# Sorting edges by node on one core: three of five comparisons on VectorE, ScalarE's comparisons earlier, and a folding of weights in sixteen steps

## The chip, the cores and the metric

The kernel runs on one core of a Trainium2 chip. The metric is the device time of one execution in microseconds (us); the figure for a kernel is the median of several executions. The core has five engines with a queue of instructions each, which they work off in order: PE (TensorE, matrix products; the loads of its stationary operand are listed apart as PEld), DVE (VectorE), ACT (ScalarE), POOL (GpSimd) and SP (SyncE, here only an issuer of transfers). Transfers run on 16 DMA engines beside them.

## The reference

A graph with 6250 nodes and 206250 edges. Every edge row of 128 numbers is added to the row of its source node; node rows, sums and one global row go through three layers with softplus between; the input is added and each row is normalised.

```python
edge_aggr = jnp.zeros((n, HIDDEN), dtype=x.dtype).at[row].add(edge_features)
global_expand = jnp.repeat(global_feat, reps, axis=0)
combined = jnp.concatenate([x, edge_aggr, global_expand], axis=-1) @ W_c + b_c
h = jax.nn.softplus(combined @ W1 + b1)
h = jax.nn.softplus(h @ W2 + b2)
return h @ W3 + b3
...
x = _layernorm(x + _L0_gnn_ref(x, edge_index, edge_attr_128, ...))
```

## The kernel before

**What is done.** The edges are sorted by source node in order to be summed with dense products. The nodes fall into 32 buckets of 196. The edges stand in 1692 columns of 122 (846 pairs of columns). For each column a one-hot matrix `sort_hot` is made that moves each of its edges to a slot; PE multiplies it with the edge rows (`gather`, line 1153, into a PSUM bank `sorted`), ScalarE copies the product into one of six sets of pairs (`settle`, line 1165), and GpSimd scatters one pair at a time to a table in device memory ordered by bucket, `rows_by` (`scatter_row`, line 1182, an indirect DMA of 256 rows). Once enough scatters are through, a chunk of 128 rows of one bucket is certain to be full: SP loads it back (`chunks`, line 293), VectorE compares its node numbers with 0 to 195 (`match`, `hot`, line 990), and PE multiplies chunk and `hot` and adds up in a PSUM tile `part` (`product`, line 1013), which VectorE adds to the sums (`sums_t`, line 1036). After the last scatter the last chunks of all buckets are summed, and the three node layers run bucket range by bucket range (lines 1356 to 1437).

**Pieces.** The 846 pairs stand in eight groups (28, 72, 124, 124, 124, 128, 124 and 122 pairs), and each group in pieces of up to three pairs, 286 pieces in all. A piece has up to six columns. Its `sort_hot` is made by one of two engines: VectorE compares all six columns in one operation (line 1137; one operand, `slot_ps`, lies in PSUM), ScalarE takes one operation a column, the distance |slot - place| (line 1140), and a last one over all six, relu(1 - distance) (line 1142). The slots themselves come from VectorE and PE, a group ahead (`positions`, lines 498 to 764).

**What sets the order.** PE, VectorE, ScalarE and SP run in an order written out by hand. Every step is entered with a nominal time and the steps are then issued in order of that time: `SCATTER` = 1.3 places is a scatter, so a piece of three pairs begins 3.9 places after the one before. For a piece that begins at t, VectorE's comparison is entered at t - 17.5 (`COMPARED`), ScalarE's operations at t - 17.5 - `SPREAD` and then every 0.65 places, PE's products at t - 14 and t - 12.05, and ScalarE's copies at t - 10.5 and t - 8.55. The nominal times give only the order; when a step runs is decided by its engine's queue and by the data. An engine whose next step waits does nothing else.

**Buffers.** `sort_hot` has three buffers, given out in the order in which the comparisons are issued; `hot` has six; the banks `sorted` three, `small` two and `part` two; the sets of pairs six; the loaded chunks six.

**The folding.** Weights and biases are multiplied out once (`node_rows`): `fold`, the first layer's weights for node rows and sums; `z_bias`, `b2_c` and `b3_all`, the three layers' biases. The bias chain has four small products, each needing VectorE's result of the one before. Two steps, `combine` and `biases`, hold all of it; `over` spreads them over the last 15% of the fourth group.

Of the kernel before, what the change touches and what calls it, by code (L numbers as in the profile page):

```python
# [7 lines left out]
F32 = mybir.dt.float32  # L8
# [6 lines left out]
ALU = mybir.AluOpType  # L15
# [3 lines left out]
P = 128  # L19
# [127 lines left out]
def kernel(  # L147
# [21 lines left out]
    nc = tc.nc  # L169
    N, D = n_nodes, x.shape[2]  # L170
# [89 lines left out]
    ones = const.tile([P, P], F32, name="ones")  # L260
# [9 lines left out]
    cols = of_weights["cols"]  # L270
# [45 lines left out]
    def small_bank():  # L316
        return ps.tile([P, 4, P], F32, name="small", bufs=2)

    with ExitStack() as phase:
        rows_p = phase.enter_context(tc.tile_pool(name="rows", bufs=ROWS))  # L320
        sort_p = phase.enter_context(tc.tile_pool(name="sort", bufs=3))
        pairs_in = phase.enter_context(tc.tile_pool(name="pairs_in", bufs=2))
        per = phase.enter_context(tc.tile_pool(name="per", bufs=2))
        keep = phase.enter_context(tc.tile_pool(name="keep", bufs=1))
# [740 lines left out]

        def node_rows():

            steps = []

            def combine():  # L1070


                small = small_bank()
                nc.tensor.matmul(small[:, 0, :1], of_weights["wc2"], cols[:, 3:4],
                                 start=True, stop=True)
                nc.vector.tensor_add(c_bias, small[:, 0, :1], cols[:, 0:1])
                small = small_bank()
                for k in range(2):
                    nc.tensor.matmul(small[:, k, :], of_weights[f"wc{k}"], w_sb["w1"],
                                     start=True, stop=True)  # L1080
                nc.vector.tensor_copy(fold, small[:, :2, :])

            def biases():
                small = small_bank()
                nc.tensor.matmul(small[:, 0, :1], w_sb["w1"], c_bias, start=True, stop=True)
                nc.vector.tensor_add(z_bias, small[:, 0, :1], cols[:, 1:2])

                nc.vector.tensor_scalar(neg_z, z_bias, -1.0, None, op0=ALU.mult)
                small = small_bank()
                nc.tensor.matmul(small[:, 0, :1], w_sb["w2"], z_bias, start=True, stop=True)  # L1090
                nc.vector.tensor_add(b2_c, small[:, 0, :1], cols[:, 2:3])
                nc.vector.tensor_scalar(neg_b2, b2_c, -1.0, None, op0=ALU.mult)
                b2_all = per.tile([P, P], F32, name="b2_all", bufs=1)
                nc.vector.tensor_scalar(b2_all, ones, b2_c, None, op0=ALU.mult)
                small = small_bank()
                nc.tensor.matmul(small[:, 0, :], b2_all, w_sb["w3"], start=True, stop=True)
                nc.vector.tensor_add(b3_all, small[:, 0, :], of_weights["b3"])
# [33 lines left out]
        def compare(i):  # L1131
            g, c, m = pieces[i]
            slot, at = slot_of[g], 2 * (c - groups[g][0])
            assert all((g, at + j) in slots_done for j in range(2 * m))
            hot = hot_of[i] = sort_p.tile([P, 2 * PAIRS, P], F32, name="sort_hot")
            if i % SHARE == 0:
                return [lambda: nc.vector.tensor_tensor(  # L1137
                    hot[:PN, :2 * m], slot[:PN, at:at + 2 * m].unsqueeze(2).to_broadcast([PN, 2 * m, P]),
                    slot_ps[:PN].unsqueeze(1).to_broadcast([PN, 2 * m, P]), op=ALU.is_equal)]
            return [lambda j=j: nc.scalar.activation(  # L1140
                hot[:PN, j], by_slot[:PN], AF.Abs, bias=slot[:PN, at + j:at + j + 1], scale=-1.0)
                for j in range(2 * m)] + [lambda: nc.scalar.activation(  # L1142
                    hot[:PN, :2 * m], hot[:PN, :2 * m], AF.Relu, bias=1.0, scale=-1.0)]
# [50 lines left out]
        with tc.manual_schedule(engines={ET.PE, ET.DVE, ET.Activation, ET.SP}):  # L1194
# [71 lines left out]
            for i, t in enumerate(begins):  # L1266
                mine = units(i)
                soon = 0.0 if i else SOON
                if i % SHARE == 0:
                    when(t - COMPARED - soon, lambda i=i: compare_next(i))  # L1270
                else:
                    for j in range(2 * pieces[i][2] + 1):
                        when(t - COMPARED - SPREAD + j * SCATTER / 2, lambda i=i: compare_next(i))
                for u, unit in enumerate(mine):
                    late_by = SCATTER * pieces[i][2] * u / len(mine)
                    soon = 0.0 if i or u else SOON
                    when(t - GATHERED + late_by - 1.7 * soon, lambda unit=unit: gather(unit))
                    when(t - SETTLED + late_by, lambda unit=unit: settle(unit))
# [338 lines left out]
```

## Time and profile before

| | us |
|---|---|
| median of 3 executions (1283.15 to 1290.0) | 1289.03 |
| the profiled execution | 1289.92 |
| its span | 1288.2 |

Busy time in that span: PE 1167.7 us (91%), DVE 1027.6 (80%), ACT 1003.9 (78%), POOL 880.9 (68%); the mean granted TensorE clock was 0.962 of full speed. The rows of the profile name source line, engine and operation, then the output tile, an arrow and the inputs. A "group" gives busy time and mean length of one, and the idle time of that engine just before it with what ended it. One product of 32-bit numbers appears as two records of PE. A "wait" row gives total us, number of times, and the longest. Idle time of an engine that nobody waits for costs nothing, and a busy PE may be a PE whose products are drawn out.

### The profile page before, as it was taken

The page shows a single profiled execution, that of the slowest core. Times are in us where ns is not written, and L with a number is a line of the kernel's source. Part 1 is how long each engine was busy: PE and PEld are TensorE (multiplying, and loading weights), DVE is VectorE, ACT ScalarE, POOL GpSimd, SP SyncE. Part 2 cuts the span into 40 slices and gives each one's busy share as a digit, 9 for nine tenths or more (in the row PEclk, how much of TensorE's full clock was granted, in tenths as well). Part 3 has the DMA queues.
Part 4 walks back from the last instruction along what each step waited for, and adds up shares of the span by engine and source line. Part 5 has one row for each costly group of instructions (what it writes and reads, how often), then busy time and mean ns, then how long its engine had stood idle before and what let it go on. Part 6 is the DMA issues. An engine that isn't in the chain of part 4 may idle for free.

```text
span 1288.2 us, 26304 instructions
## 1 busy us (share of the span) xinstructions
PE 1167.7 (91%) x8617; PEld 1111.8 (86%) x8617; DVE 1027.6 (80%) x2260; ACT 1003.9 (78%) x2335; POOL 880.9 (68%) x915
## 2 busy tenths in 40 slices
PE   5778898888998998999899999999999999899893
PEld 5667788877988898989899999999999999898772
DVE  7868977888789977899878887789876767687784
ACT  5897987899687888977998888988899999403343
POOL 2777777777577776776777777777777777750334
PEclk9788998989999998999999999999999999999996
DMA  6789998899999997997999999999999999874421
GB/s 248 240 296 347 344 334 288 305 344 355 339 327 331 362 330 278 319 325 246 322 309 309 323 336 328 345 313 335 316 350 334 369 336 363 288 218 140 140 75 53
DMA packets 174636, 381.96 MB, mean 297 GB/s; under 512 B 27546, under 2 KB 118626, under 8 KB 160670
## 3 DMA queue, kind: packets, MB, share of 16 engines
q1 hardware_dynamic: 130751, 260.70, 61.2%
q0 software_dynamic: 41328, 115.65, 23.1%
q10 hardware_dynamic: 2415, 3.85, 0.9%
q8 instruction: 72, 1.18, 0.4%
q14 instruction: 70, 0.57, 0.1%
HBM read 242.47 MB, written 142.20 MB: 299 GB/s over the span
## 4 chain that ended last, share of the span: by engine, by line
PE 65%; DVE 12%; ACT 8%; DMA 7%; issue 4%; POOL 3%; SPq 0%; ACTq 0%; DVEq 0%; POOLq 0%
PE part L1013 37%; PE sorted L1153 21%; ACT pairs L1165 4%; DMA rows_by<-pairs,pair 4%; POOL rows_by L1182 3%; ACT sort_hot L1140 3%; DMA chunks<-rows_by 3%; DVE hot L990 2%; DVE past L727 1%; PE small L557 1%; PE small L559 1%; ACT sort_hot L1142 1%; DVE sort_hot L1137 1%; DVE sums_t L1036 1%; PE small L1395 1%
## 5 line engine op out<-in xcount | busy, mean ns | idle before, releaser
L1182 POOL DMA_INDIRECT rows_by<-pairs,pair x846 | 828.1, 979 | 298.3 <-issue 202.8
L1013 PE MATMUL part<-hot,chunks 128*128 128x196 f32 x3516 | 675.1, 335 | 13.2 <-DVE sums_t L1036 9.9
L1165 ACT COPY pairs<-sorted 64x387 f32<-64x387 f32 (+2 forms) x1144 | 542.6, 474 | 118.8 <-PE sorted L1153 95.7
L1013 PEld LDWEIGHTS part<-hot,chunks 128*128 128x128 f32 x3516 | 582.0, 193 | 21.9 <-DVE sums_t L1036 11.3
L1153 PE MATMUL sorted<-rows,sort_hot 122*128 122x129 f32 x3384 | 498.5, 288 | 44.5 <-ACT sort_hot L1142 32.0
L1153 PEld LDWEIGHTS sorted<-rows,sort_hot 122*128 122x128 f32 x3384 | 457.6, 199 | 53.5 <-ACT sort_hot L1142 36.3
L990 DVE TENSOR_TENSOR hot<-chunks,both_ps 128x784 f32<-128x784 f32 (+3 forms) x541 | 426.1, 809 | 9.2 <-DMA chunks<-rows_by 9.0
L1140 ACT ACTIVATE sort_hot<-plain,slot 122x128 f32<-122x128 f32 x840 | 292.8, 394 | 18.6 <-PE sorted L1153 6.3
L1036 DVE TENSOR_TENSOR sums_t<-sums_t,part 128x392 f32<-128x392 f32 (+1 forms) x262 | 143.5, 548 | 134.0 <-PE part L1013 133.0
L1137 DVE TENSOR_TENSOR sort_hot<-slot,both_ps 122x768 f32<-122x768 f32 x143 | 134.5, 940 | 1.9 <-PE sorted L1153 1.0
L1142 ACT ACTIVATE sort_hot<-sort_hot 122x768 f32<-122x768 f32 x143 | 118.6, 830 | 3.9
L1437 POOL TENSOR_SCALAR y<-y,mv,rs 128x128 f32<-128x128 f32 x40 | 31.1, 785 | 93.8 <-DVE rs L1425 93.5
L576 DVE TENSOR_REDUCE slot<-small 122x16 f32<-122x512 f32 (+2 forms) x109 | 72.9, 668 | 21.5 <-PE small L559 20.7
L1367 ACT ACTIVATE away<-sorted,z_bias 128x512 f32<-128x512 f32 (+2 forms) x13 | 8.5, 656 | 72.9 <-PE sorted L1357 72.9
L498 DVE TENSOR_TENSOR pair_ib<-pair_block,plain 122x512 bf16<-122x512 bf16 (+2 forms) x157 | 63.4, 411 | 0.2
L557 PE MATMUL small<-pair_ib,half 122*122 122x512 bf16 (+2 forms) x109 | 43.3, 398 | 7.6 <-DVE slot L576 7.5
L742 PEld LDWEIGHTS <-past 128*128 128x128 f16 x424 | 25.4, 100 | 17.9 <-DVE past L727 12.7
L727 DVE TENSOR_TENSOR past<-both_ps,starts 128x512 f16<-128x512 f32 (+1 forms) x61 | 39.8, 664 | 1.2 <-PE small L742 0.9
L742 PE MATMUL small<-jump,past 128*128 128x56 f16 (+3 forms) x424 | 29.4, 190 | 11.8 <-DVE past L727 8.4
L559 PEld LDWEIGHTS <-starts_h 128*122 128x122 bf16 x236 | 25.3, 148 | 11.9 <-issue 7.7
L1114 ACT COPY rows<-pair_i 122x16 f32<-122x16 f32 x106 | 22.2, 209 | 17.0 <-DMA rows<-in_edge 16.4
L727 DVE TENSOR_TENSOR past<-both_ps,starts_late 128x512 f16<-128x512 f32 (+2 forms) x49 | 32.3, 661 | 0.0
(163 smaller groups left out, 515.6 us busy)
## 6 DMA issues: line engine op xcount, KB each, us to landing
rows<-in_edge SPq DMA_DIRECT2D x105, 1032.0 KB
chunks<-rows_by SPq DMA_DIRECT2D x362, 136.0 KB
chunks<-rows_by SPq DMA_DIRECT2D x203, 204.0 KB
chunks<-rows_by SPq DMA_DIRECT2D x75, 272.0 KB
rows_by<-pairs,pair POOLq DMA_INDIRECT x846
rows_by<-fill SPq DMA_DIRECT2D x10, 1249.5 KB
rows_by<-fill SPq DMA_DIRECT2D x10, 714.0 KB
chunks<-rows_by SPq DMA_DIRECT2D x13, 408.0 KB
```

The source lines that it names most:

```text
L498: nc.vector.tensor_tensor(ib, cols.unsqueeze(2).to_broadcast([PN, m, SB, QUAD]), bucket_at[:PN].unsqueeze(1).to_broadcast([PN, m, SB, QUAD ...
L576: nc.vector.tensor_reduce(to, of, axis=mybir.AxisListType.X, op=ALU.max)
L727: nc.vector.tensor_tensor(past[:, :, a:b], twice_ps[:KB].unsqueeze(1).unsqueeze(1).to_broadcast([KB, 2, b - a, P // 2]), own["starts"][:, ...
L990: nc.vector.tensor_tensor(hot[:, q - a:q - a + m], chunks[j][:, lo:hi + 1:step, D:W].to_broadcast([P, m, BL]), iota_ps.unsqueeze(1).to_bro ...
L1013: nc.tensor.matmul(part[:, b - base_of[v], :], t[:, place_in(j, q), :D], hot[:, q - a], start=first, stop=last)
L1036: nc.vector.tensor_add(here, here, of)
L1137: return [lambda: nc.vector.tensor_tensor(hot[:PN, :2 * m], slot[:PN, at:at + 2 * m].unsqueeze(2).to_broadcast([PN, 2 * m, P]), slot_ps[:P ...
L1140: return [lambda j=j: nc.scalar.activation(hot[:PN, j], by_slot[:PN], AF.Abs, bias=slot[:PN, at + j:at + j + 1], scale=-1.0) for j in rang ...
L1142: for j in range(2 * m)] + [lambda: nc.scalar.activation(hot[:PN, :2 * m], hot[:PN, :2 * m], AF.Relu, bias=1.0, scale=-1.0)]
L1153: nc.tensor.matmul(out[:, j, :], hot[:PN, at], rows_at[col // LOAD_COLS][:PN, col % LOAD_COLS, :], start=True, stop=True)
L1165: nc.scalar.copy(sets_at[i][64 * n:64 * n + 64, lo:lo + m, h, :W], out[64 * h:64 * h + 64, :m, :])
L1182: s = nc.gpsimd.indirect_dma_start(out=dst, out_offset=bass.IndirectOffsetOnAxis(ap=at, axis=0), in_=rows[:, j].rearrange("p a b -> p (a b ...
```

## The change

A few numbers and one function change. `BY_ACT` = (1, 3) of `SHARE` = 5: of five pieces the second and fourth are compared by ScalarE and the other three by VectorE, where the engines took turns. `SPREAD` grows from 2.0 to 4.5, so that ScalarE's operations are entered 22 places ahead of the piece. `sort_hot` gets a fourth buffer, `hot` gives up its sixth. The folding is cut into sixteen steps, three of them empty.

```diff
-SHARE, SPREAD = 2, 2.0
+BY_ACT, SHARE, SPREAD = (1, 3), 5, 4.5
...
-    hots = ctx.enter_context(tc.tile_pool(name="hots", bufs=6))
+    hots = ctx.enter_context(tc.tile_pool(name="hots", bufs=5))
...
-        sort_p = phase.enter_context(tc.tile_pool(name="sort", bufs=3))
+        sort_p = phase.enter_context(tc.tile_pool(name="sort", bufs=4))
...
-            return [combine, biases]
+            banks_of, v = {}, nc.vector
+
+            def product_of(name, *pairs):
+                small = banks_of[name] = small_bank()
+                for k, (of, by, w) in enumerate(pairs):
+                    nc.tensor.matmul(small[:, k, :w], of, by, start=True, stop=True)
+
+            def got(name, k=0, w=1):
+                return banks_of[name][:, k, :w]
...
+            return [
+                lambda: product_of("c", (of_weights["wc2"], cols[:, 3:4], 1)),
+                lambda: product_of("fold", *((of_weights[f"wc{k}"], w_sb["w1"], D) for k in range(2))),
+                lambda: v.tensor_add(c_bias, got("c"), cols[:, 0:1]),
+                lambda: v.tensor_copy(fold, banks_of["fold"][:, :2, :]),
+                lambda: product_of("z", (w_sb["w1"], c_bias, 1)),
+                lambda: None,
+                lambda: v.tensor_add(z_bias, got("z"), cols[:, 1:2]),
+                lambda: v.tensor_scalar(neg_z, z_bias, -1.0, None, op0=ALU.mult),
+                lambda: product_of("b2", (w_sb["w2"], z_bias, 1)),
+                lambda: None,
+                lambda: v.tensor_add(b2_c, got("b2"), cols[:, 2:3]),
+                lambda: v.tensor_scalar(neg_b2, b2_c, -1.0, None, op0=ALU.mult),
+                b2_rows,
+                lambda: product_of("b3", (b2_all[0], w_sb["w3"], D)),
+                lambda: None,
+                lambda: v.tensor_add(b3_all, got("b3", w=D), of_weights["b3"]),
+            ]
...
-            if i % SHARE == 0:
+            if i % SHARE not in BY_ACT:
...
-                if i % SHARE == 0:
+                if i % SHARE not in BY_ACT:
                     when(t - COMPARED - soon, lambda i=i: compare_next(i))
```

How this moves the instructions, at two places. ScalarE, in the middle of the scatter stage (`pairs_108` to `pairs_113` are the six sets; a piece has four copies, its comparison six operations that read `plain` and `slot` and a last one on `sort_hot` alone); before:

```order
L1165 COPY pairs_110<-sorted 64x3x129 x4
L1114 COPY rows<-pair_i 122x16
L1140 ACTIVATE sort_hot<-plain,slot 122x128 x2
L1165 COPY pairs_111<-sorted 64x3x129 x2
L1140 ACTIVATE sort_hot<-plain,slot 122x128 x3
L1165 COPY pairs_111<-sorted 64x3x129 x2
L1140 ACTIVATE sort_hot<-plain,slot 122x128
L1142 ACTIVATE sort_hot<-sort_hot 122x768
L1165 COPY pairs_112<-sorted 64x3x129 x4
```

and with the change (lines are two higher):

```order
L1167 COPY pairs_111<-sorted 64x3x129 x2
L1116 COPY rows<-pair_i 122x16
L1167 COPY pairs_112<-sorted 64x3x129 x2
L1142 ACTIVATE sort_hot<-plain,slot 122x128 x3
L1167 COPY pairs_112<-sorted 64x3x129 x2
L1142 ACTIVATE sort_hot<-plain,slot 122x128 x3
L1167 COPY pairs_113<-sorted 64x3x129 x2
L1144 ACTIVATE sort_hot<-sort_hot 122x768
L1167 COPY pairs_113<-sorted 64x3x129 x2
L1167 COPY pairs_108<-sorted 64x3x129 x4
```

The comparison that stood among the copies of one piece now begins among those of one piece and ends among those of the next, and there are pieces whose copies follow with no comparison between.

PE at the folding; before:

```order
L1074 MATMUL small<-weights_sb 128x1
L1079 MATMUL small<-weights_sb 128x128 x2
L1153 MATMUL sorted<-rows,sort_hot 128x129 x3
L1013 MATMUL part<-hot,chunks 128x196 x4
L1153 MATMUL sorted<-rows,sort_hot 128x129 x2
L1013 MATMUL part<-hot,chunks 128x196 x4
L1153 MATMUL sorted<-rows,sort_hot 128x129 x6
L1013 MATMUL part<-hot,chunks 128x196 x7
L1153 MATMUL sorted<-rows,sort_hot 128x129 x9
L1085 MATMUL small<-c_bias,weights_sb 128x1
L1090 MATMUL small<-z_bias,weights_sb 128x1
L1096 MATMUL small<-weights_sb,b_all 128x128
```

and with the change, from the third small product on:

```order
L1073 MATMUL small<-c_bias,weights_sb 128x1
L1155 MATMUL sorted<-rows,sort_hot 128x129 x3
L1013 MATMUL part<-hot,chunks 128x196 x4
L1155 MATMUL sorted<-rows,sort_hot 128x129 x2
L1013 MATMUL part<-hot,chunks 128x196 x4
L1155 MATMUL sorted<-rows,sort_hot 128x129 x6
L1013 MATMUL part<-hot,chunks 128x196 x3
L1073 MATMUL small<-z_bias,weights_sb 128x1
L1013 MATMUL part<-hot,chunks 128x196 x4
L1155 MATMUL sorted<-rows,sort_hot 128x129 x12
L1073 MATMUL small<-weights_sb,b_all 128x128
```

The three products of the bias chain stood back to back and now have sixteen or more other products between them. The orders of SP and GpSimd are the same as before.

More of the change, by code (lines that the diff above doesn't have):

```diff
@@ L1066, in node_rows @@
         def node_rows():
[L1068 to L1097, printed above, removed]
@@ L1099, in node_rows, with b2_rows @@
-            return [combine, biases]
+            banks_of, v = {}, nc.vector
[5 more added lines that the diff above has]
+                return banks_of[name][:, k, :w]
+            b2_all = []
+            def b2_rows():
+                b2_all.append(per.tile([P, P], F32, name="b2_all", bufs=1))
+                v.tensor_scalar(b2_all[0], ones, b2_c, None, op0=ALU.mult)
```

## The prediction, made before the changed kernel ran

> **What bounds the kernel now.** I read the page, then the waits of each engine, the stretches of 50 us, and last the order of time where a wait ended late. The page's groups give the prices:
>
> ```profile
> span 1288.2 us, 26304 instructions
> L1182 POOL DMA_INDIRECT rows_by<-pairs,pair x846 | 828.1, 979 | 298.3 <-issue 202.8
> L1140 ACT ACTIVATE sort_hot<-plain,slot 122x128 f32<-122x128 f32 x840 | 292.8, 394 | 18.6 <-PE sorted L1153 6.3
> L1137 DVE TENSOR_TENSOR sort_hot<-slot,both_ps 122x768 f32<-122x768 f32 x143 | 134.5, 940 | 1.9 <-PE sorted L1153 1.0
> L1142 ACT ACTIVATE sort_hot<-sort_hot 122x768 f32<-122x768 f32 x143 | 118.6, 830 | 3.9
> ```
>
> The scatters are one queue of 846 on GpSimd. Their line's instructions and the waits before them:
>
> ```profile
> L1182 POOL DMA_INDIRECT rows_by<-pairs,pair x846: 971/972/1407, 22.1 to 1127.0; - x170
> POOL rows_by L1182 <- issue: 202.8, 663, 0.6
> POOL rows_by L1182 <- DMA rows_by<-pairs,pair: 33.0, 78, 6.4
> POOL rows_by L1182 <- ACT pairs L1165: 23.9, 51, 2.1
> POOL rows_by L1182 <- ACT sort_hot L1140: 7.3, 20, 1.5
> POOL rows_by L1182 <- ACT sort_hot L1142: 3.7, 12, 0.3
> ```
>
> A scatter takes 0.971 us and the shortest idle ahead of the next is 0.30 us, so the queue cannot go below 1.271 us a pair: 845 x 1.271 = 1074 us from first start to last. It took 1104.9 us, 31 us more. Idle above the floor of 0.30 us is 3.9 (issue) + 9.6 (DMA) + 8.6 + 1.3 + 0.1 (data that ScalarE had not settled); the rest, some 7 us, is longer scatters (mean 979). So the scatter stage is bound by GpSimd to within 3%, and only the 10 us of "not settled" can be won by better comparisons. The stretches say where (columns: busy and count of PE, weight loads, DVE, ACT, POOL; clock; DMA share; GB/s):
>
> ```profile
> 50.00:100.00 50.00, 38.65 (x315) 35.31 (x315) 35.42 (x92) 47.57 (x114) 38.11 (x40) 0.81 0.81 281
> 100.00:150.00 50.00, 41.60 (x348) 38.28 (x347) 47.59 (x118) 42.23 (x101) 38.11 (x40) 0.95 0.93 336
> 300.00:350.00 50.00, 46.08 (x342) 44.71 (x341) 37.28 (x73) 40.39 (x97) 31.62 (x33) 0.93 0.98 343
> 400.00:450.00 50.00, 46.31 (x380) 44.74 (x379) 47.65 (x106) 40.98 (x95) 37.20 (x38) 0.97 0.97 350
> 563.00:630.00 67.00, 60.94 (x507) 58.22 (x506) 65.40 (x150) 52.70 (x124) 48.09 (x50) 1.00 0.85 299
> 650.00:700.00 50.00, 50.00 (x379) 49.09 (x378) 41.29 (x73) 45.01 (x106) 38.10 (x40) 1.00 0.94 316
> 1000.00:1050.00 50.00, 50.00 (x358) 50.00 (x357) 34.97 (x47) 46.70 (x110) 38.10 (x40) 1.00 1.00 358
> ```
>
> Forty scatters in 50 us is the full rate. From 650 us to the end of the scatters GpSimd runs at it and PE has no gap: they are balanced there. Before, PE has gaps, above all for the comparisons that ScalarE makes, and hardly any for VectorE's:
>
> ```profile
> PE sorted L1153 <- ACT sort_hot L1142: 32.0, 23, 2.2
> PE sorted L1153 <- ACT pairs L1165: 8.8, 12, 3.6
> PE sorted L1153 <- DVE sort_hot L1137: 2.3, 2, 1.9
> ```
>
> Yet in 50 to 150 us, where ScalarE is busiest and PE waits most, GpSimd loses nothing. PE's lateness reaches the end only where GpSimd runs dry, and in the tail.
>
> **The change part by part.** *Shares.* Of 286 pieces VectorE compares 172 instead of 143, ScalarE 114 instead of 143. ScalarE loses 29 final operations of 118.6 / 143 = 0.83 us and 156 single comparisons of 292.8 / 840 = 0.349 us: 24.1 + 54.4 = 78.5 us. VectorE gains 29 x 0.941 = 27.3 us. Both are in the scatter stage and neither engine sets its end, so what counts is GpSimd's hunger. *Earlier comparisons.* 2.5 places more of head start, with a fourth buffer so that this does not wait for the product. A buffer is now taken by a piece's ScalarE comparison ahead of the VectorE comparison of the piece before it; the closest case is a VectorE comparison whose buffer's last product lies 2.4 places ahead of it, so I cost that at nothing, hidden while PE is less than 2.4 places late; if PE is later the VectorE operation waits as long as PE is late beyond that. The long gaps of GpSimd:
>
> ```profile
> 229.66 0.97 POOL L1182 DMA_INDIRECT rows_by<-pairs,pair  x1 [1.89 <-ACT pairs L1165]
> 340.12 0.97 POOL L1182 DMA_INDIRECT rows_by<-pairs,pair  x1 [6.35 <-DMA rows_by<-pairs,pair]
> 500.65 0.97 POOL L1182 DMA_INDIRECT rows_by<-pairs,pair  x1 [2.07 <-ACT pairs L1165]
> 505.50 0.97 POOL L1182 DMA_INDIRECT rows_by<-pairs,pair  x1 [1.28 <-ACT pairs L1165]
> 587.66 0.97 POOL L1182 DMA_INDIRECT rows_by<-pairs,pair  x1 [1.21 <-ACT pairs L1165]
> ```
>
> Seven gaps from the one at 587.66 to 614 us add 4.0 us above the floor; they lie in the stretch 563 to 630, where VectorE is busy 65.4 of 67 us and ScalarE only 52.7. These are VectorE's. The remaining 6 us (229, 304, 428, 500, 505 us) are ScalarE's, or the folding's. I take all 6 us off (bounds 0 and -6). In the VectorE stretch 67 / 3.82 us = 17.5 pieces bring 1.75 more VectorE comparisons, +1.7 us; against that the chain enters it with more settled pairs, which I let cover half of the 4.0: together -0.3 (bounds -4 and +5, the latter if the stretches at 100 and 400 us, as full, each pay another 1.7).
>
> *Folding in sixteen steps.* Now PE and VectorE answer one another at one place:
>
> ```profile
> 484.77 0.28 PE L1085 MATMUL small<-c_bias,weights_sb 128*128 128x1 f32 x2
> 485.09 0.16 DVE L1086 TENSOR_TENSOR z_bias<-small,weights_sb 128x1 f32<-128x1 f32 x1 [4.48 <-PE small L1085]
> 495.10 2.98 PE L1013 MATMUL part<-hot,chunks 128*128 128x196 f32 x8 [3.58 <-DVE sums_t L1036]
> ```
>
> VectorE stood 4.48 us for PE's small product, was late with the next comparisons and node codes, and PE then stood 3.58 us; GpSimd's gaps at 500.65 and 505.50 follow. With a step between a product and its reader, and two before the dependent product, the wait goes; it is the 2.75 us above the floor of those two gaps, already in the 6 us. No instruction is added, and no DMA or queue of SP or GpSimd moves. If the spacing is too short at PE's real pace, the 4.48 us is paid again in parts.
>
> *The tail.* PE's order after its last sort product, and from the chain of waits one load of chunks:
>
> ```profile
> 1109.67 0.61 PE L1153 MATMUL sorted<-rows,sort_hot 122*128 122x129 f32 x4
> 1122.87 1.59 PE L1013 MATMUL part<-hot,chunks 128*128 128x196 f32 x8 [0.60 <-DVE sums_t L1036]
> 1127.95 28.81 PE L1013 MATMUL part<-hot,chunks 128*128 128x196 f32 x162 [3.49 <-DVE sums_t L1036]
> 1156.60 1.02 PE L1356 MATMUL sorted<-x_t,fold 128*128 128x512 f32 x2
> 1112.97 6.29 DMA chunks<-rows_by
> ```
>
> PE is the bound from here. The first layer product at 1156.60 needs buckets 0 to 2, whose last visits hold 29 chunks, 58 records; 104 of the 162 records therefore do not need the last scatter, 104 x 28.81 / 162 = 18.5 us, so the first product on the last scatter's rows starts near 1146. Its rows could be ready at 1127.0 + 0.97 + about 3 for landing + 6.3 for a load like the one at 1112.97 + 1 for its match = 1138. So PE may be up to 8 us further ahead of GpSimd than now and still gain. PE's waits of 32.0 us make the lead easily, but pairs can be settled only six pieces ahead of GpSimd, and at 1109.67 PE already led by (1127.0 - 1109.67) / 1.271 = 13.6 of those 18 pairs, which leaves 4.4 x 1.271 = 5.6 us. I take -4 (bounds 0 and -8). *Five buffers for matches* instead of six let VectorE run one unit less ahead; no match waits for a buffer now. 0 to +3 (the 1.59 us of eight records at two of the tail's waits); I take +0.5. *Start.* Three comparisons now lie between the two halves of the first piece's copies, of which the second half ended 0.3 us before the first scatter:
>
> ```profile
> 20.86 0.97 ACT L1165 COPY pairs<-sorted 64x387 f32<-64x387 f32 x2 [0.69 <-PE sorted L1153]
> ```
>
> 3 x 0.349 less the wait of 0.69 that they fill is +0.4 (0 to +1).
>
> Sum: -6 - 0.3 - 4 + 0.5 + 0.4 = -9.4. The profiled execution took 1289.92 us (span 1288.2 and 1.7 around it), 0.9 above the median of 1289.03: 1280.5, or **1279.6** against the median.
>
> **The rivals.** *No change.* GpSimd is fed already, and where it is not, DMA is the reason: 9.6 us of its gaps are DMA's, the share is 0.98 in 300 to 350 and 1.00 in 1000 to 1050. Then only the folding's 2.75 us goes, less the start's 0.4, and a scatter that lands late stops PE through the six sets as before: 1289.0 - 2.4 = 1286.6. Against it: the five gaps that end on ScalarE's copies. The Trainium skill, DMA: Bandwidth & Descriptors, section "Queues, rings and completion order", has each DMA engine take turns between queues by packets; by it a scatter among chunk loads lands late however early its data is, which is this rival; the share of 0.98 beside the gap of 6.35 us agrees.
>
> *Slower: VectorE becomes the bound.* After the change it is busier than ScalarE in the scatter stage. Its added 27.3 us would be on the path wherever it is full while it prepares the next group's positions; if that is the whole time up to 650 us, 27.3 x 650 / 1128 = 15.7 us, less the 6 us saved: about 1298.7. It decides from the point at which VectorE is busy over 47 of 50 us, as in three of thirteen stretches now; against it, the 2.3 us that PE waits for VectorE's comparisons, and 35 to 42 us of busy time in most stretches.
>
> *Much faster.* PE's stops also slow its clock and hold back SP's loads, which wait for its buffers:
>
> ```profile
> 315.00:320.00 5.00, 2.11 (x15) 1.54 (x13) 2.48 (x7) 4.36 (x13) 3.80 (x4) 1.00 0.92 331
> 320.00:325.00 5.00, 4.25 (x16) 4.25 (x17) 4.30 (x8) 4.88 (x13) 3.89 (x4) 0.51 0.93 301
> SPq L293 <- PE part L1013: 400.9, 175, 7.7
> ```
>
> After 2.9 us without work the granted clock is 0.51. Without the stops loads spread out, the 9.6 us of DMA gaps go too, and the tail wins its 8 us: -9.4 - 9.6 - 4 = -23, 1266. The Trainium skill, TensorE: Matmul & The Clock Gate, section "Part 1: The HAM clock gate", says that a PE idle for a window of about 3.4 us falls to half clock until it has been busy for another; the row agrees.
>
> **How the numbers follow.** Forecast 0.52, no change 0.21, VectorE bound 0.09, much faster 0.18. A measurement of this kernel tells about 0.5%, 6.4 us, from no change: faster means below 1282.6. The forecast lies 3 us below that and its terms move by that much, so I give three quarters of it to faster: 0.39 + 0.18 + 0.01 = 0.58. Same: 0.13 + 0.19 + 0.01 = 0.33. Slower: 0.09. Range: 1267, near the much faster case, to 1291, which takes in no change with the start's and the matches' upper ends and leaves out most of the slower case.
>
> **What would show it.** Right: PE's wait for ScalarE's comparisons falls from 32 us below 8; GpSimd's waits for ScalarE's copies fall from 23.9 us, 51 times, towards the floor; no wait of over 1 us at z_bias; the last scatter starts near 1121 and the first layer product near 1147. VectorE's share rises by 27 us, ScalarE's falls by 78. Wrong: the last scatter still near 1127 with larger DMA waits (no change); GpSimd dry in 100 to 150 and 400 to 450 us beside a VectorE that is full, or PE waiting for VectorE's sort_hot by more than 10 us (slower).

## The result and the profile after

| kernel | median, us | executions | lowest to highest |
|---|---|---|---|
| before | 1287.18 | 6 | 1283.15 to 1290.0 |
| changed | 1280.91 | 6 | 1280.05 to 1282.52 |

The ratio is 0.9954, interval [0.9934, 0.9974]. It is worked out from all executions, so ratios here can differ by 0.1% from the quotient of two medians. The medians lie 6.3 us apart: a small gain, but the interval leaves out 1. The profiled pair exaggerates it: 1289.92 us, near the slowest execution of before, against 1280.91. The span of the changed kernel's profiled execution was 1279.1 us. Its line numbers are two higher than those shown of before: scatters 1184, copies into the sets (`settle`) 1167, sort products 1155, ScalarE's comparisons 1142 and 1144, VectorE's 1139.

The page of the changed kernel, its busy times and the groups that answer to those shown of before (busy us, mean ns of one, then the idle time ahead and what ended it):

```profile
span 1279.1 us, 26170 instructions
PE 1156.0 (90%) x8617; PEld 1098.4 (86%) x8617; DVE 1047.0 (82%) x2289; ACT 913.4 (71%) x2150; POOL 883.6 (69%) x915
...
L1142 ACT ACTIVATE sort_hot<-plain,slot 122x128 f32<-122x128 f32 x684 | 227.9, 392 | 8.8 <-DVE slot L576 5.9
L1139 DVE TENSOR_TENSOR sort_hot<-slot,both_ps 122x768 f32<-122x768 f32 (+2 forms) x172 | 159.6, 928 | 7.7 <-PE sorted L1155 7.4
L1144 ACT ACTIVATE sort_hot<-sort_hot 122x768 f32<-122x768 f32 x114 | 95.9, 841 | 0.2
```

The shares moved as the change says: 172 comparisons on VectorE, 114 on ScalarE. ScalarE is 90.5 us less busy, VectorE 19.4 us more. The scatter line of the changed kernel (shortest, median and longest ns; first and last start):

```profile
L1184 POOL DMA_INDIRECT rows_by<-pairs,pair x846: 972/976/1292, 22.5 to 1120.5; - x170
```

The last scatter starts 6.5 us earlier than before, at 1120.5. The waits of the changed kernel (total us, times, longest):

```profile
POOL rows_by L1184 <- issue: 208.1, 682, 0.6
POOL rows_by L1184 <- DMA rows_by<-pairs,pair: 30.2, 75, 3.2
POOL rows_by L1184 <- ACT pairs L1167: 19.9, 56, 1.9
...
ACT pairs L1167 <- DMA rows_by<-pairs,pair: 41.2, 21, 6.5
PE sorted L1155 <- ACT pairs L1167: 25.3, 34, 3.9
PE sorted L1155 <- DVE sort_hot L1139: 10.2, 4, 5.2
DVE sort_hot L1139 <- PE sorted L1155: 7.4, 4, 3.2
```

Read it from the bottom of the pipe. GpSimd's idle above its floor of 0.30 us was 8.6 us for ScalarE's copies and is 19.9 - 56 x 0.30 = 3.1; for DMA it was 9.6 and is 30.2 - 75 x 0.30 = 7.7. PE's 32.0 us of waiting for ScalarE's comparisons have left the list. In their place stand two others. ScalarE's copies wait 41.2 us, where it was 3.3, for a set of pairs to come free, because all six are full and an old scatter has not landed. And PE waits 25.3 us for ScalarE's copies, where it was 8.8; added up from the order of time, only 4.0 of these fall into time in which ScalarE itself waits for a set, and in some 20 of them it is making copies. So the sets are not the main reason for PE's waits, but they now cut off part of the lead. How that looks in order of time is seen at 296 us, where the longest wait for a set ends (start, length, engine, instruction, idle before):

```profile
296.54 0.97 ACT L1167 COPY pairs<-sorted 64x387 f32<-64x387 f32 x2 [6.49 <-DMA rows_by<-pairs,pair]
296.65 0.97 POOL L1184 DMA_INDIRECT rows_by<-pairs,pair  x1 [3.17 <-DMA rows_by<-pairs,pair]
297.56 1.66 PE L1155 MATMUL sorted<-rows,sort_hot 122*128 122x129 f32 x6 [3.94 <-ACT pairs L1167]
299.26 0.95 DVE L1139 TENSOR_TENSOR sort_hot<-slot,both_ps 122x768 f32<-122x768 f32 x1 [3.21 <-PE sorted L1155]
```

The wait for one scatter to land stops ScalarE for 6.49 us, then PE for 3.94, and VectorE for 3.21, since its `sort_hot` buffer still waits for PE's product. GpSimd lost 3.17 us there, not the 6.35 us that it lost once before at 340. The stretch around it, and the one in which VectorE is fullest (columns as in the prediction):

```profile
250.00:300.00 50.00, 37.65 (x301) 35.62 (x301) 42.10 (x117) 35.89 (x86) 34.78 (x35) 0.89 0.96 354
...
563.00:630.00 67.00, 62.57 (x512) 59.67 (x511) 64.40 (x123) 48.47 (x116) 50.93 (x53) 1.00 0.86 298
```

In the first, with a DMA share of 0.96, PE is busy 37.65 of 50 us and GpSimd starts 35 scatters, not 40. The kernel before started 39 there at the same share; its own long wait for DMA came one stretch later, at 340 us. In the second VectorE is no busier than before (65.40), and GpSimd starts 53 scatters instead of 50.

The tail, PE's order after its last sort product:

```profile
1101.64 0.61 PE L1155 MATMUL sorted<-rows,sort_hot 122*128 122x129 f32 x4
...
1115.49 1.59 PE L1013 MATMUL part<-hot,chunks 128*128 128x196 f32 x8 [1.26 <-DVE sums_t L1036]
1120.21 27.39 PE L1013 MATMUL part<-hot,chunks 128*128 128x196 f32 x162 [3.12 <-DVE sums_t L1036]
1147.44 1.02 PE L1358 MATMUL sorted<-x_t,fold 128*128 128x512 f32 x2
```

The first layer product is 9.2 us earlier than before (1156.60). Of this 6.5 us are the last scatter's and 1.5 a longer lead: at the last sort product PE leads GpSimd by (1120.5 - 1101.64) / 1.271 = 14.8 pairs, where it led by 13.6. The remaining 1.1 us lie between the last sort product and the first layer product, 45.8 us for 46.9: the 162 records behind the second stop take 27.39 us for 28.81. In the kernel before, the granted clock was 0.95 from 1120 to 1130 us and 0.88 from 1130 to 1140; in the changed one it stays at 1.00. The stops, 0.60 and 3.49 us before, are 1.26 and 3.12. From the first layer product to the end of the span nothing changed (131.6 and 131.7 us).

### The profile page after: what moved, and what is told of

The parts are those of the page before. It is cut to its first block, busy times and chain, and to the rows that moved or that the text cites. A ratio compares the mean times of both kernels' runs of the same rounds, so it can differ in the third digit from the quotient of the medians.

```text
span 1279.1 us, 26170 instructions
## 1 busy us (share of the span) xinstructions
PE 1156.0 (90%) x8617; PEld 1098.4 (86%) x8617; DVE 1047.0 (82%) x2289; ACT 913.4 (71%) x2150; POOL 883.6 (69%) x915
## 4 chain that ended last, share of the span: by engine, by line
PE 62%; DVE 11%; DMA 11%; ACT 6%; issue 5%; POOL 4%; SPq 0%; ACTq 0%; DVEq 0%; POOLq 0%
PE part L1013 37%; PE sorted L1155 20%; DMA rows_by<-pairs,pair 7%; POOL rows_by L1184 4%; ACT pairs L1167 3%; DMA chunks<-rows_by 3%; DVE hot L990 2%; ACT sort_hot L1142 1%; PE small L557 1%; PE small L559 1%; DVE past L727 1%; DVE sort_hot L1139 1%; PE small L1397 1%; PE sorted L1362 1%; DVE slot L576 1%
## 5 line engine op out<-in xcount | busy, mean ns | idle before, releaser
L1155 PE MATMUL sorted<-rows,sort_hot 122*128 122x129 f32 x3384 | 489.6, 284 | 36.3 <-ACT pairs L1167 25.3
L1155 PEld LDWEIGHTS sorted<-rows,sort_hot 122*128 122x128 f32 x3384 | 448.9, 196 | 45.7 <-ACT pairs L1167 35.7
L1142 ACT ACTIVATE sort_hot<-plain,slot 122x128 f32<-122x128 f32 x684 | 227.9, 392 | 8.8 <-DVE slot L576 5.9
L1139 DVE TENSOR_TENSOR sort_hot<-slot,both_ps 122x768 f32<-122x768 f32 (+2 forms) x172 | 159.6, 928 | 7.7 <-PE sorted L1155 7.4
L1144 ACT ACTIVATE sort_hot<-sort_hot 122x768 f32<-122x768 f32 x114 | 95.9, 841 | 0.2
L742 PEld LDWEIGHTS <-past 128*128 128x128 f16 x424 | 24.7, 98 | 22.6 <-DVE past L727 17.8
```

Of the source, the lines that this page charges most:

```text
L1139: return [lambda: nc.vector.tensor_tensor(hot[:PN, :2 * m], slot[:PN, at:at + 2 * m].unsqueeze(2).to_broadcast([PN, 2 * m, P]), slot_ps[:P ...
L1142: return [lambda j=j: nc.scalar.activation(hot[:PN, j], by_slot[:PN], AF.Abs, bias=slot[:PN, at + j:at + j + 1], scale=-1.0) for j in rang ...
L1144: for j in range(2 * m)] + [lambda: nc.scalar.activation(hot[:PN, :2 * m], hot[:PN, :2 * m], AF.Relu, bias=1.0, scale=-1.0)]
L1155: nc.tensor.matmul(out[:, j, :], hot[:PN, at], rows_at[col // LOAD_COLS][:PN, col % LOAD_COLS, :], start=True, stop=True)
```

## The experiments

The theory of the prediction credits **feeding**: ScalarE carries less, is less late, and GpSimd is fed. Its rival is **head start**: only when ScalarE's comparisons are entered counts. A second one is **folding**, and for the tail **lead**: how far the sets let PE run ahead. Runs of one job share the kernel before on the same chip; ratios are to it. "Share alone" and "head start alone" both carry the change's buffers, four for comparisons and five for matches; the head start without the fourth buffer was not run.

### The parts one by one

**Folding alone**: the kernel before with the sixteen-step `node_rows` and nothing else of the change.

```diff
-            return [combine, biases]
+            return [
+                lambda: product_of("c", (of_weights["wc2"], cols[:, 3:4], 1)),
...
```

> The kernel before with the folding in sixteen steps alone; comparisons, head start and buffers as before. Feeding theory (the gain comes from GpSimd being fed by a less loaded ScalarE, the folding is worth its two gaps of 2.75 us at most): 1 to 3 us under the kernel before, PE's wait for ScalarE's comparisons still near 32 us, no wait of over 1 us at z_bias. Folding theory (VectorE's stop of 4.48 us and what follows it is the whole gain): 5 to 7 us under the kernel before.

**Share and buffers alone**: old folding, old head start.

```diff
-BY_ACT, SHARE, SPREAD = (1, 3), 5, 4.5
+BY_ACT, SHARE, SPREAD = (1, 3), 5, 2.0
```

> Three of five comparisons on VectorE with the buffers of the change (four for comparisons, five for matches), head start of ScalarE as before (19.5 places), folding in two steps. Feeding theory: ScalarE's 78 us less work is what counts, PE's wait for ScalarE's comparisons falls from 32 us below 12, 3 to 5 us under the kernel before. Head-start theory (ScalarE's work was early enough in sum, but began too late): PE's wait stays over 20 us and the time within 2 us of the kernel before.

**Head start and buffers alone**: old folding, the engines take turns.

```diff
-SHARE, SPREAD = 2, 2.0
+SHARE, SPREAD = 2, 4.5
```

> ScalarE's comparisons 22 places ahead with the buffers of the change, engines still taking turns, folding in two steps. Head-start theory: PE's wait for ScalarE's comparisons falls below 12 us and the time is 3 to 5 us under the kernel before. Feeding theory: ScalarE, busy 45 of 50 us, is late however early its work is entered; the wait stays over 15 us and the time within 2.5 us of the kernel before.

**The change with the old folding.**

```diff
-            return [
-                lambda: product_of("c", (of_weights["wc2"], cols[:, 3:4], 1)),
...
+            return [combine, biases]
```

> The changed kernel with the folding in two steps as before. Feeding theory: the pairs that lead GpSimd cover VectorE's stop of some 4.5 us, so at most 2.5 us over the changed kernel, and PE's wait for ScalarE's comparisons stays near zero. Folding theory: 5 us or more over the changed kernel, that is the time of before.

A later job added the missing combination, **head start and folding without the share**:

```diff
-BY_ACT, SHARE, SPREAD = (1, 3), 5, 4.5
+BY_ACT, SHARE, SPREAD = (1,), 2, 4.5
```

> The changed kernel with the engines taking turns at the pieces again (SHARE 2); 22 places, four and five buffers and the sixteen steps stay. Head-start theory (the head start alone frees PE of ScalarE, the shares add nothing to the time): within 2 us of the changed kernel, some 6 us under the kernel before, PE's wait for ScalarE's comparisons under 3 us. Feeding theory (ScalarE's smaller load is needed): 3 us or more over the changed kernel, PE's wait over 10 us.

Measured (the kernel before took 1288.38 us, 29 executions, beside the first four, and 1287.62, 23 executions, beside the last):

| kernel | share | head start | folding | median, us | ratio to before |
|---|---|---|---|---|---|
| folding alone | | | new | 1283.78 | 0.9960 [0.9943, 0.9978] |
| share alone | new | | | 1287.26 | 0.9986 [0.9969, 1.0004] |
| head start alone | | new | | 1281.89 | 0.9947 [0.9926, 0.9968] |
| without folding | new | new | | 1283.71 | 0.9963 [0.9947, 0.9979] |
| without share | | new | new | 1277.97 | 0.9923 [0.9899, 0.9947] |
| changed | new | new | new | 1280.91 | 0.9954 [0.9934, 0.9974] |

The share alone does nothing that can be told, and the other parts are as good without it as with it (0.9947 and 0.9963, 0.9923 and 0.9954; their intervals overlap). The head start alone brings the whole gain. Folding alone lands at 4.6 us, between the two ranges expected (1 to 3 and 5 to 7). Folding and head start bring 0.40% and 0.53% alone and 0.77% together, which within the intervals is their sum: these two parts add. With the share on top it is 0.46%. Whether the share costs something there is not told, as the last two intervals overlap. Without the share the median lies 2.9 us under the changed kernel's, where head start had expected within 2 and feeding 3 or more over it. Without folding it lies 2.8 us over, 1.2 by the ratios, about the 2.5 that feeding had allowed and far from the 5 of folding.

The waits of the kernel with the share alone, where ScalarE's load is lighter and its head start the old one:

```profile
POOL rows_by L1182 <- ACT pairs L1165: 31.1, 71, 2.7
...
PE sorted L1153 <- ACT sort_hot L1142: 19.4, 18, 2.2
```

ScalarE is busy 931.7 us instead of 1003.9. PE still waits 19.4 us for its comparisons, and GpSimd's idle for copies above its floor is 31.1 - 71 x 0.30 = 9.8 us, not less than the 8.6 of before. The 19.4 us are a little less than the 20 that head start had forecast as the least, and well over the 12 of feeding. The kernel with the head start alone:

```profile
POOL rows_by L1182 <- ACT pairs L1165: 23.3, 55, 2.1
ACT pairs L1165 <- DMA rows_by<-pairs,pair: 23.0, 20, 5.5
PE sorted L1153 <- ACT pairs L1165: 29.1, 41, 2.9
...
DVE z_bias L1086 <- PE small L1085: 4.4, 1, 4.4
```

Here all comparisons of before are ScalarE's again, and PE's wait for them is off the list all the same, since they are entered earlier. The folding's 4.4 us at `z_bias` still stands, and the sets are full now and then (23.0 us). So the feeding theory falls by the times: how early ScalarE's comparisons stand in the order decides, not how many there are. By which wait the head start works is less clear. Much of PE's wait has moved from comparisons to copies (29.1 us, 8.8 before), and PE's waits for ScalarE in all fell as far with the share alone, 19.4 + 8.4 = 27.8 us, as with the head start alone, 29.1, from 32.0 + 8.8 = 40.8.

For where the gain came from, GpSimd's idle ahead of scatters, less 0.30 us each, was added up from the order of time by stretch, and by what ended it (A: ScalarE's results, D: a DMA; stretches before 100 and after 630 us have none but the first scatters' 20 us and are left out). The last three rows are, from the same profiles, the start of the last scatter, PE's lead over GpSimd at the last sort product, worked out as above, and the time of the profiled execution. One profiled execution each:

| us from the start | before | folding alone | share alone | head start alone | without folding | without share | changed |
|---|---|---|---|---|---|---|---|
| 100 to 400, A | 2.8 | 3.1 | 0.6 | 0.4 | 1.1 | 0.2 | 0.1 |
| 400 to 480, A | 0.8 | 5.2 | 4.7 | 2.2 | 0.3 | 1.7 | 2.6 |
| 480 to 560, A | 2.8 | 0.0 | 1.2 | 0.6 | 0.0 | 0.0 | 0.0 |
| 560 to 630, A | 3.8 | 1.3 | 4.3 | 3.9 | 0.6 | 0.6 | 0.2 |
| all, A | 10.2 | 9.6 | 10.8 | 7.1 | 2.0 | 2.5 | 2.9 |
| all, D | 9.3 | 5.2 | 5.0 | 4.9 | 9.2 | 5.0 | 7.4 |
| last scatter, us | 1127.0 | 1122.2 | 1124.1 | 1120.6 | 1119.4 | 1115.1 | 1120.5 |
| lead, pairs | 13.6 | 12.8 | 13.0 | 15.0 | 13.5 | 12.9 | 14.8 |
| execution, us | 1289.92 | 1287.18 | 1286.46 | 1283.75 | 1280.66 | 1277.81 | 1280.91 |

Folding alone takes 2.8 + 2.5 us away where it stands and just behind it, which suggests that the stall of VectorE had been felt up to 630 us. But 4.4 us came up ahead of it, at 400 to 480, and of the 4.8 us by which its last scatter is earlier, 4.1 are DMA's gaps; so where its gain of 4.6 us comes from is not shown. Two parts together empty the stretch 560 to 630 (0.2 to 0.6 us), while share alone and head start alone each leave it as it was. DMA's gaps are 5 to 9 us with no order in the parts, so 4 us of the difference between two single profiles says nothing of the change.

The kernel without the share, the fastest of these, shows that a longer lead is not needed for a gain:

```profile
L1184 POOL DMA_INDIRECT rows_by<-pairs,pair x846: 971/972/1224, 22.2 to 1115.1; - x170
```
```profile
1098.65 0.61 PE L1155 MATMUL sorted<-rows,sort_hot 122*128 122x129 f32 x4
```

Its last scatter starts 11.9 us earlier than before, with 7.7 us less of A and 4.3 of D, while its lead of 12.9 pairs is shorter than the 13.6 of before.

### The lead that the sets allow

**Five sets of pairs in the changed kernel**, and **ScalarE with one piece in five**, for the question whether VectorE is near its limit.

```diff
-SETS = 6
+SETS = 5
```

> The changed kernel with five sets of pairs in place of six, on a chip on which the kernel before takes its usual time. Lead theory: PE's lead over GpSimd at the last scatter is three pairs, 3.8 us, less and the tail longer by as much; ScalarE's wait for scatters rises from 41 us above 70; 3 to 7 us over the changed kernel. Hunger theory: within 2 us of the changed kernel.

```diff
-BY_ACT, SHARE, SPREAD = (1, 3), 5, 4.5
+BY_ACT, SHARE, SPREAD = (2,), 5, 4.5
```

> Four of five comparisons on VectorE, 53 us more of it, on a chip on which the kernel before takes its usual time. Slack theory (VectorE waits for PE over 110 us): within 3 us of the changed kernel. VectorE-bound theory: 8 us or more over it.

| kernel | median, us | ratio to before |
|---|---|---|
| five sets | 1286.51 | 0.9998 [0.9983, 1.0012] |
| four of five on VectorE | 1282.81 | 0.9962 [0.9944, 0.9979] |

Both stand beside the kernel before of 1287.62 us. With five sets the whole gain is gone: 0.44% over the changed kernel, 5.7 us, within the 3 to 7 expected. The waits, the scatter line and PE's order of the kernel with five sets:

```profile
ACT pairs L1167 <- DMA rows_by<-pairs,pair: 78.2, 42, 5.3
```
```profile
L1184 POOL DMA_INDIRECT rows_by<-pairs,pair x846: 972/976/1296, 22.5 to 1123.6; - x170
```
```profile
1111.00 0.61 PE L1155 MATMUL sorted<-rows,sort_hot 122*128 122x129 f32 x4
...
1156.70 1.02 PE L1358 MATMUL sorted<-x_t,fold 128*128 128x512 f32 x2
```

The profiled execution was the slowest of the twelve, 1290.08 us, so it lies 9.2 us over the changed kernel's where the medians lie 5.6 apart. The wait for a set almost doubles. At the last sort product PE leads by (1123.6 - 1111.00) / 1.271 = 9.9 pairs instead of 14.8, and the first layer product is back at 1156.70, 9.3 us later than in the changed kernel, of which the last scatter accounts for 3.1. Three pairs less in the sets are 3 x 1.271 = 3.8 us, and the lead fell by 4.9 pairs or 6.2 us. So in the changed kernel the sixth set is worth as much as the whole change, by the lead and by GpSimd's supply. That the gain comes from the lead is not shown by it: the kernel before was not run with five sets and may lose as much, and the kernel without the share gained more with a shorter lead.

Four of five on VectorE makes it 67 us busier than before and changes nothing that can be told from the changed kernel: 1.9 us, within the 3 expected of slack and far from the 8 of a bound VectorE. Its busy times and PE's wait for VectorE:

```profile
PE 1162.0 (91%) x8617; PEld 1105.5 (86%) x8617; DVE 1094.8 (85%) x2346; ACT 762.6 (60%) x1745; POOL 882.2 (69%) x915
```
```profile
PE sorted L1155 <- DVE sort_hot L1139: 14.4, 6, 4.9
```

The wait for VectorE grows from 10.2 to 14.4 us, and in 560 to 630 us, worked out as in the table above, 3.3 us of gaps are back. So VectorE's load may show in that stretch once it has one further piece in five, but at some 3 us in one profile and not 15.

### The tail's stops

When ScalarE has made its last copy it issues the loads of all node rows for the layers in one go, while SP's last chunks are being loaded. Here they go out two steps ahead of their use instead, three tiles at the start, with GpSimd's additions to them moved along.

```diff
-            for n0, w in tiles:
+            def rows_of_x(n0, w):
                 x_of[n0] = node_rows_of(ahead, n0, w, len(tiles), load=nc.scalar.dma_start)
...
             for step in range(len(tiles) + 2):
...
+                for k in {0: (0, 1, 2)}.get(step, (step + 2,)):
+                    if k < len(tiles):
+                        rows_of_x(*tiles[k])
```

> The changed kernel with the tail's loads of node rows spread over the layers' steps, on a chip on which the kernel before takes its usual time. If these loads delay the chunk loads at the end of the scatters: PE's stops of 1.3 and 3.1 us go, 3 to 6 us under the changed kernel. If the chunk loads wait for the scatters and for each other: within 1.5 us.

It took 1272.52 us (4 executions, 1271.81 to 1275.66), ratio 0.9883 [0.9858, 0.9908]: faster than the changed kernel, whose interval begins at 0.9934, and by 8.4 us between the medians, over the 3 to 6 expected. In the changed kernel, ScalarE's queue (start, time to the last issue; the first of the fifteen loads had been issued at 1102.35) and two stretches of the tail (columns as in the prediction):

```profile
1102.73 20.54 ACTq L306 DMA_DIRECT2D x_sb<-in_x  x14
```
```profile
1110.00:1120.00 10.00, 5.83 (x34) 5.22 (x32) 5.79 (x9) 0.00 (x0) 7.62 (x8) 1.00 1.04 396
1120.00:1130.00 10.00, 9.79 (x57) 9.49 (x58) 7.48 (x13) 0.00 (x0) 9.61 (x9) 1.00 0.89 284
```

The same stretches, and PE's order, of the kernel with the later loads:

```profile
1110.00:1120.00 10.00, 9.45 (x57) 9.15 (x56) 9.60 (x16) 0.00 (x0) 7.76 (x9) 1.00 0.99 324
1120.00:1130.00 10.00, 10.00 (x62) 10.00 (x61) 8.66 (x15) 0.00 (x0) 2.78 (x3) 1.00 0.65 187
```
```profile
1115.30 27.13 PE L1013 MATMUL part<-hot,chunks 128*128 128x196 f32 x162 [0.55 <-DVE sums_t L1036]
1142.27 1.02 PE L1358 MATMUL sorted<-x_t,fold 128*128 128x512 f32 x2
```

PE works 19.45 of these 20 us instead of 15.62. The wait of VectorE's matches for chunks, 7.7 us six times in the changed kernel, is 0.2 us once. The chain that ended last runs in the changed kernel through two loads of chunks there, of 7.02 us from 1104.93 and 6.61 from 1111.97, and with the later loads through none. GpSimd's additions, which the edit moves too, cannot have made the stops: in the changed kernel they begin at 1121.6, when both are over. From the last sort product (1100.84) to the first layer product it takes 41.4 us instead of 45.8: 4.4 us shown. Most of it is the two stops of 1.26 and 3.12, of which one of 0.55 is left. The profiled executions lie 5.2 us apart (1275.66 and 1280.91), the rest of which is the scatter stage's; the profiled one was the slowest of four, so the other 3 us of the 8.4 between the medians are not seen in any trace.

### Runs that told nothing

One job held the kernel with five sets, the one with four of five, the one with later loads, and one with seven sets, for which another match buffer was given up:

```diff
-SETS = 6
+SETS = 7
...
-    hots = ctx.enter_context(tc.tile_pool(name="hots", bufs=5))
+    hots = ctx.enter_context(tc.tile_pool(name="hots", bufs=4))
```

> The changed kernel with seven sets of pairs, the room taken from matches (four buffers, not five). Lead theory: ScalarE's wait for scatters falls below 25 us, 2 to 4 us under the changed kernel. Hunger theory: within 1.5 us, or slower by what the fourth match buffer costs in the tail.

> The changed kernel with five sets of pairs in place of six, so that settled pairs can lead GpSimd by 15, not 18. Lead theory (with the change PE is held back by the sets, and its lead at the last scatter is part of the gain): ScalarE's wait for scatters rises from 41 us above 70, the time is 3 to 7 us over the changed kernel. Hunger theory (only the gaps in which GpSimd has nothing to scatter count): within 2 us of the changed kernel.

> The changed kernel with four of five comparisons on VectorE (229 pieces in place of 172, 57 x 0.93 = 53 us more of VectorE, 57 x 2.8 = 160 us less of ScalarE). Slack theory (VectorE has room, it waits for PE over 110 us): within 4 us of the changed kernel. VectorE-bound theory: 10 us or more over it, GpSimd dry in the stretches in which VectorE prepares the next group.

> The changed kernel, with the tail's loads of node rows (3.1 MB, which ScalarE issues all at once when its copies end) spread over the layers' steps, three tiles ahead. Theory that these loads delay the chunk loads at the end of the scatters, where PE stops for 1.3 and 3.1 us: both stops go, 3 to 6 us under the changed kernel. Theory that the chunk loads wait for the scatters and for each other: the stops stay, within 1.5 us.

In that job every kernel took 24% longer, the kernel before included: 1596.95 us (35 executions). Ratios there: seven sets 1.0003 [0.9969, 1.0036], five sets 0.9966 [0.9936, 0.9996], four of five 0.9958 [0.9930, 0.9987], later loads 0.9977 [0.9947, 1.0006]. The waits of the kernel with five sets in that job:

```profile
POOL rows_by L1184 <- ACT pairs L1167: 302.6, 118, 6.7
...
ACT pairs L1167 <- remote: 162.3, 47, 7.0
```

GpSimd idled 302.6 - 118 x 0.30 = 267 us above its floor there, and its scatters took 0.97 us as ever (the last began at 1423.0); ScalarE waited for something that the profile cannot name. With GpSimd dry for that long, and for a reason that the profile does not name, these runs test neither theory, and three of the kernels were measured again in the job told above. What slowed that job is not settled. Seven sets were run only there, so whether more lead brings more stays open.

## Why the prediction was right, point by point

- **Size and end.** Forecast 1279.6, measured 1280.91. In part this is luck: the gain was forecast at 9.4 us from a median of 1289.03, and it is 6.3 us from 1287.18, the median of twice as many executions. In the profiled pair the forecast fits better, 9.0 us. For the parts, last scatter forecast near 1121, found at 1120.5; first layer product near 1147, found at 1147.44. The reading that carried this holds: GpSimd's 1.271 us a pair bounds the stage, only its hunger can be won, and the tail gives a little more.
- **The -6 us.** Right in sum, by two errors that cancel: ScalarE's gaps fell from 10.2 to 2.9 us, 7.3 where -6 and the stretch's -0.3 were forecast, but outside 560 to 630 us they fell by 3.7 (from 6.4 to 2.7) and not 6, and inside by 3.6 and not 0.3. Wrong in cause. The term was built on the 78.5 us taken from ScalarE ("Both are in the scatter stage ... so what counts is GpSimd's hunger"); the share alone left PE's wait at 19.4 us and the time as it was, while the head start alone, with no load taken away, removed that wait, though much of it came back at the copies, and brought 0.53%. Of the forecasts, "PE's wait ... falls from 32 us below 8" was met by a part of the change to which the text had given only a sentence.
- **VectorE's stretch, 563 to 630.** I let the added comparisons cost 1.7 us and better supply cover half of the 4.0; nearly all of the 3.8 us vanished. The reading "These are VectorE's" was too short: folding alone brings them to 1.3, which suggests that part was VectorE's stall at `z_bias`, felt 100 us later. With four of five on VectorE 3.3 us come back. Each is one profile.
- **Folding.** The 4.48 us wait at `z_bias` went as forecast; the longest new one, at the next bias, is 1.02 us. Its price of 2.75 us was too low for folding alone (about 4.6 us); why is open, as told above. On top of share and head start it cannot be told from nothing (0.9963 against 0.9954), nor on top of the head start alone (0.9947 against 0.9923).
- **The tail's -4.** Right in direction: the first layer product came 2.6 us earlier in relation to the last scatter. The reason given holds for 1.5 of them, a lead longer by 1.2 pairs; 1.1 are the tail's own products, which I had not priced. With one set fewer the lead and the whole gain went. I had not asked why PE stopped twice in the tail; those stops were priced only as a risk of the fifth match buffer, and they were the loads of node rows.
- **Five match buffers, +0.5, and the start, +0.4.** Neither can be separated. VectorE's matches now wait 3.1 us for PE to free a buffer, and the first scatter starts at 22.5 instead of 22.1, but with the old head start (folding alone) it started at 22.6 as well.
- **The buffers' order at nothing.** I said that VectorE waits as long as PE is late beyond 2.4 places. PE is that late now: 7.4 us of VectorE's waits, four times, and 10.2 us of PE's for VectorE, over the 10 us that I had named as the sign of the slower case. No price shows at the end: PE waited for VectorE at 67, 156, 256 and 291 us, while GpSimd's gaps of over 0.5 us for ScalarE's copies stand at 417, 438, 455 and 607. That sign was badly chosen: a wait of PE says nothing while the queue behind it holds pairs.
- **Busy times.** VectorE +19.4 for +27, ScalarE -90.5 for -78. VectorE's comparisons alone took 159.6 - 134.5 = 25.1 us more; ScalarE's comparisons took 87.6 us less, not 78.5, because a single comparison takes less busy time, 227.9 / 684 = 0.333 us for 0.349. One still lasts 392 ns, for 394; more of it overlaps with its neighbour.
- **The rivals.** *No change* had half of the truth: DMA's gaps stayed (9.6 to 7.7 us), and the sets fill. The rule of the Trainium skill, DMA: Bandwidth & Descriptors, section "Queues, rings and completion order", that a DMA engine takes turns between queues by packets, agrees with the 3.17 us at 296.65 and the DMA share of 0.96 in 250 to 300 us, where the scatter's data had long been settled; no run here tells this rule from another cause of late landing. *VectorE as bound* falls: 67 us more on it than before still gave 0.9962. *Much faster* asked for DMA's 9.6 us to go and they did not, but its other half, the tail's stops, was there to be had by another edit. Its reading of the clock was too simple: behind the "2.9 us without work" stand two waits of PE, 1.38 us up to 317.58 and 2.23 us up to 320.75, with 0.94 us of products between them. The granted clock was then 0.50 from 321 to 326 us, so it fell to half here without an idle window of 3.4 us in full.

## What to carry to other kernels

Where engines work off fixed orders and one queue at the end sets the pace, look first at how early a late step is entered, and only then at how much work its engine has: 2.5 places of head start, with the buffer that goes with it, did what 72 us less work did not. Do not read the worth of a part off one engine's waits: PE's waits for ScalarE fell as far in the kernel that gained nothing. Look at the ring of buffers in front of the paced queue too: one set less cost the changed kernel its whole gain. And try a change without each of its parts: the kernel without the share was at least as fast. When an engine runs out of work at the end of a stage, look at what it issues next all at once: spreading those loads brought more than the change itself, and the best kernel here is the changed one with that edit, 1272.52 us.

## What was not expected of the hardware

- Fifteen loads of node rows, some 3.1 MB issued within 21 us beside the chunks, went with a DMA share of 1.04 in 1110 to 1120 us and cost PE, which needs none of them yet, 4.4 us; with three tiles ahead the share there was 0.99 and then 0.65 where it had been 0.89.
- The same kernel took 1287.62 us in one job and 1596.95 in another, with scatters of the same 0.97 us (the mean granted clock of the kernel with five sets was 0.970 in the one and 0.904 in the other): the waits ahead of the scatters differed, not their length. The trace names no cause.
- The median scatter was 0.972 us in eleven of the fourteen profiles and 0.976 in three: the changed kernel, the one with seven sets, and the one with five, which in the slow job was at 0.972. Over 846 scatters that is 3 us, which no edit explains.
